# A four-layer graph network on one core: the program's end, the last group's gate and the due times of the planner rearranged

## The chip, the core and the metric

The kernel runs on one core of a Trainium2 chip. Its engines are TensorE (PE, with its weight loads shown apart as PEld), VectorE (DVE), ScalarE (ACT), GpSimd (POOL) and SyncE (SP), which issues the DMAs. The metric is the device time of one execution in microseconds. The kernel before takes 2499.73 us, the median of three runs (2499.19 to 2499.82).

## The reference

Input: 128 graphs of 64 nodes with 256 features (`x`), a 0/1 adjacency for each graph (`adj`) and a node mask. Four layers follow each other; each is `x = x + gnn(relu(layernorm(x)))`, and the layernorm has no weights of its own. Cut to what matters:

```python
# layers 0 and 1: attention, 8 heads of 32, masked by adj
scores = einsum('bhqd,bhkd->bhqk', q, k) / sqrt(32)        # layer 1 adds log(adj + 1e-6) instead
attn = softmax(where(adj > 0, scores, NEG))
out = merge_heads(attn @ v) @ Wo + bo
# layer 2: five GRU steps on h
for l in range(5):
    agg = A.T @ (h @ weight[l])
    r, z, n = gates(agg @ w_ih.T + b_ih, h @ w_hh.T + b_hh)
    h = (1 - z) * n + z * h
# layer 3: a gate between a neighbour part and an own part
f_hom = (adj @ ((x @ theta) * norm)) * norm                # norm = degree ** -0.5
f_het = x @ W_h
gate = sigmoid(x @ W_t + b_t)
out = elu(gate * f_hom + (1 - gate) * f_het)
```

All of it is float32.

## The kernel before, in words

Two graphs make a pair of 128 rows (tokens on the partitions); four pairs make a group, and there are 16 groups. For each group the function `front` computes layers 0 and 1 (in two halves of two pairs), `entry` and `gru` the five steps of layer 2 on all four pairs, and `back` (with `back_half` at L1453 for each half) layer 3. Dense products of two halves use a scheme with seven products in place of eight; the weights' combinations are made once at the start. Small products inside a graph (scores `s`, attention times values `o`, aggregation `agg`) use parts of the PE array: 64x64 or 64x32 tiles. Full products and transposes use all of it.

Nothing is issued in the order of the program text. Each operation is first added to a `Plan` with its engine, a cost in ns, what it reads and writes, and a due time. `plan.strand(base, span)` spreads the due times of the operations added in it evenly by PE cost over `base` to `base + span`, counted in groups. `Plan.run` then simulates five engine clocks and takes, again and again, the operation that can start first; among those that can start within 15 ns of the first it takes the one due first. Three sets of constants steer this:

- `AFTER`, `TO_PE`, `TO_POOL` and `EASE` say how long after an operation's end its result is there for another engine. `EASE` is a slack on top of all of them.
- `BESIDE`, `ALONE` and `TURNING` shift the due time of small-tile operations and transposes by the tile mode in which PE was left last (`shift`), and `AHEAD` limits how far ahead of the earliest due time an operation may be taken.
- `FRONT...`, `BACK...`, `STEP...`, `LOCK`, `ENTRY`, `FIRST...` and `FUSE...` are the bases and spans of the strands. `..._LAST` and `BACK_END` shift those of the last group or the last two, and `LOCK` starts the last group's layer 2 earlier.

The plan decides the order on each engine. On the chip each engine works through its own queue in that order and waits on semaphores.

Layer 3 in `back_half`, for each pair: the last state of layer 2 is added into `x` (L1458), `normed` makes the normalized and transposed `hT` (`lnT`, L563, is its transpose on PE; `st`, `mv`, `pw` and `rstd` are its statistics), products give `F` with three parts (L1396 and L1400 in `plain_products`: `f` on its own bank, `gate` with 512 columns for the gate and the own part). Then the bias is added to the gate (L1476 on POOL in the last group, L1479 on DVE in the others), tanh by ACT (L1481), `hom` by PE (L1483), three operations of DVE that combine the parts (L1486, L1489, L1491), the lower branch of ELU (L1497 by ACT in the last two groups, a min by DVE in the others, then exp at L1502), and two DVE operations that add both branches and the −1 into `x` (L1504, L1506). One DMA stores both pairs of the half (L1508, 256 KB).

The network exists in the program twice. The first copy (`flag` given, "lean") takes the softmax without subtracting the maximum and counts in `sure` and `once` whether that was safe (L1559 to L1577, which writes `flag`). The second copy is the fallback without this shortcut. Which one holds is decided at the end of the first (L284, L285):

```python
        network(tc, a, out, flag)
        beyond = nc.values_load(flag[0:1, 0:1])
        with tc.If(beyond > 0, preferred_fallthrough_block=False):
            network(tc, a, out, None)
```

With these inputs the fallback isn't run; each engine jumps over it. The wait for the last stores stands at the program's very end (L1607).

Of the kernel before, what the change touches and what calls it, by code (L numbers as in the profile page):

```python
# [23 lines left out]
P = 128  # L24
# [14 lines left out]

AFTER = {"PE": 210, "DVE": 125, "ACT": 145, "POOL": 90, "SP": 2500}  # L40
TO_PE, TO_POOL = 120, 60
EASE = 60


HOLD = {"DVE": 60, "POOL": 95}
# [5 lines left out]

WIDE, T64, T32, TURN = range(4)
CHANGE = ((0, 95, 95, 0), (290, 0, 170, 190), (250, 135, 30, 150), (0, 95, 95, 0))
BESIDE = 0.78
ALONE = 0.07
TURNING = 0.14
AHEAD = 1.25

FRONT = 0.1
FRONT_LAST = 0.25
FRONT_SPAN = 1.03
BACK = 0.0
BACK_LAST = 0.35
BACK_SPAN = 0.7
STEP = 0.1
STEP_LAST = -0.02
STEP_SPAN = 0.35
LOCK = 0.26  # L70
BACK_END = 0.1
ENTRY = 0.55
FIRST = -1.33
FIRST_SPAN = 1.08
ORDER = (0, 0, 1, 0, 1, 0)
FUSE = -1.25
FUSE_SPAN = 0.2


WEIGH = (655, 1147)  # L80
# [10 lines left out]
def dve(n, ptr=0):  # L91
    return n * 1.042 + 68 + 60 * ptr
# [186 lines left out]
def gnn_stack_kernel(tc: tile.TileContext, a: dict, out: bass.AP):  # L279
    nc = tc.nc  # L280
    with tc.tile_pool(name="flag", bufs=1) as keep:
        flag = keep.tile([P, 1], mybir.dt.int32, name="flag")
        network(tc, a, out, flag)
        beyond = nc.values_load(flag[0:1, 0:1])  # L284
        with tc.If(beyond > 0, preferred_fallthrough_block=False):  # L285
            network(tc, a, out, None)


# [1 line left out]
def network(ctx: ExitStack, tc: tile.TileContext, a: dict, out: bass.AP, flag):  # L290
# [38 lines left out]
    def vec2(cost, fn, reads, writes, early=0.0):  # L329

        plan.add("DVE", cost, fn, reads, writes, early=early, port=True)
# [4 lines left out]
    def pool(cost, fn, reads, writes, early=0.0, port=1):  # L336
        plan.add("POOL", cost, fn, reads, writes, early=early, port=port)
# [45 lines left out]
    def load_row(name):  # L383
        t = new(f"r_{name}", [P, D], 1)
        ap = a[name]
        dma(128, lambda: nc.sync.dma_start(
            t.tile, bass.AP(tensor=ap.tensor, offset=ap.offset, ap=[[0, P], [1, D]])), [], [t])
        return t
# [117 lines left out]
    with plan.strand(-0.3, 0.1):  # L506

        b_rz = new("b_rz", [P, 4], 1)
        vec(160, lambda: nc.vector.tensor_add(b_rz.tile, cols[:, 4:8], cols[:, 10:14]), [cols], [b_rz])
        vec(160, lambda: nc.vector.tensor_scalar(b_rz.tile, b_rz.tile, 0.5, None, op0=ALU.mult),  # L510
            [b_rz], [b_rz])


        b_n = new("b_n", [P, 2], 1)
        vec(160, lambda: nc.vector.tensor_sub(b_n.tile, cols[:, 8:10], cols[:, 14:16]), [cols], [b_n])


        w3 = new("w3", [P, 3, 8, P], 1)

        def load_w3():  # L520
            for i, name in enumerate(("L3_gnn_theta", "L3_gnn_W_t", "L3_gnn_W_h")):
                nc.sync.dma_start(w3[:, i, :4, :].rearrange("p (c o) q -> p c (o q)", c=2),
                                  a[name].rearrange("(c p) o -> p c o", p=P))

        dma(768, load_w3, [], [w3], 3)
        b_t = load_row("L3_gnn_b_t")


        b_row = new("b_row", [P, 2, 4, P], 1)
        more = new("e", [P, 2, 2, P], 4 if lean else 3, "b_more")  # L530

        def load_b():
            ih, hh = a["L2_gnn_b_ih"], a["L2_gnn_b_hh"]
            for dst, ap, at, gates in ((b_row[:, :, 0], ih, 2 * D, 0), (b_row[:, :, 3], hh, 2 * D, 0),
                                       (more[:, :, 0], hh, 0, 0), (more[:, :, 1], hh, D, 0),
                                       (b_row[:, :, 1], ih, 0, 0), (b_row[:, :, 2], ih, D, 0)):
                nc.sync.dma_start(dst, bass.AP(tensor=ap.tensor, offset=ap.offset + at, ap=[[0, P], [P, 2], [1, P]]))

        dma(768, load_b, [], [b_row, more], 6)
        pool(1225, lambda: nc.gpsimd.tensor_tensor(  # L540
            b_row[:, :, 1:3, :], b_row[:, :, 1:3, :], more.tile, op=ALU.add), [b_row, more], [b_row])
        blk = filled("adjblk", [P, PAIRS, P], 0.0)
# [911 lines left out]
    def back_half(g, xt, adjT, norm, half):  # L1454
        h_by_token = final[g]
        for p in range(2 * half, 2 * half + 2):
            t = g * PAIRS + p
            vec2(dve(256, 1), lambda t=t, p=p: nc.vector.scalar_tensor_tensor(  # L1458
                xt[:, p, :], h_by_token[:, p, :], cols[:, 18 + t : 19 + t], xt[:, p, :],
                op0=ALU.mult, op1=ALU.add),  # L1460
                [(h_by_token, ("half", half)) if g + 1 == n_groups else h_by_token, cols, (xt, p)], [(xt, p)])
        hT = normed(xt, half, f"{g}_3_{half}")

        F = [new("F" if g + 2 < n_groups or half else "h" if g + 2 == n_groups else ("kexp", "qk")[i], [P, 3, D], 2, f"F_{g}_{2 * half + i}") for i in range(2)]
        if g + 1 == n_groups or g + 2 == n_groups and not half:
            plain_products(hT, F, f"{g}_{half}")
        else:
            seven_products(hT, F, f"{g}_{half}")
        for p in range(2 * half, 2 * half + 2):
            nm = f"{g}_{p}"  # L1470
            v = F[p % 2]
            o = new("o", [P, D], 2, f"o3_{nm}")
            ph = bank(f"hom_{nm}")
            f, gt, het = (lambda k=k, v=v: v[:, k, :] for k in range(3))
            if g + 1 == n_groups:
                pool(650, lambda gt=gt: nc.gpsimd.tensor_tensor(gt(), gt(), b_t.tile, op=ALU.add),  # L1476
                     [(v, 0), (v, 1), b_t], [(v, "gt")])
            else:
                vec2(dve(256), lambda gt=gt: nc.vector.tensor_tensor(gt(), gt(), b_t.tile, op=ALU.add),  # L1479
                    [(v, 0), (v, 1), b_t], [(v, "gt")])  # L1480
            sca(act(256, 0.4), lambda gt=gt: nc.scalar.activation(gt(), gt(), AF.Tanh, scale=0.5),  # L1481
                [(v, "gt")], [(v, "gt")])
            pe(mm(256), lambda p=p, f=f, ph=ph: nc.tensor.matmul(  # L1483
                ph[:, :D], adjT[:, p, :], f(), start=True, stop=True), [adjT, (v, 0), (v, 1)], [ph], holds=[o])

            vec(dve(256, 1), lambda p=p, o=o, ph=ph, het=het: nc.vector.scalar_tensor_tensor(  # L1486
                o.tile, ph[:, :D], norm[:, p : p + 1], het(), op0=ALU.mult, op1=ALU.subtract),
                [ph, norm, (v, 0), (v, 1)], [o])
            vec2(dve(256), lambda o=o, gt=gt: nc.vector.scalar_tensor_tensor(  # L1489
                o.tile, gt(), 1.0, o.tile, op0=ALU.add, op1=ALU.mult), [(v, "gt"), o], [o])  # L1490
            vec2(dve(256), lambda o=o, het=het: nc.vector.scalar_tensor_tensor(  # L1491
                o.tile, o.tile, 0.5, het(), op0=ALU.mult, op1=ALU.add), [o, (v, 0), (v, 1)], [o])


            end = g + 2 >= n_groups
            if end:
                sca(act(256, 0.4), lambda o=o, gt=gt: nc.scalar.activation(gt(), o.tile, AF.Relu, scale=-1.0),  # L1497
                    [o], [(v, "gt")])
            else:
                vec2(210, lambda o=o, gt=gt: nc.vector.tensor_scalar(gt(), o.tile, 0.0, None, op0=ALU.min),  # L1500
                    [o], [(v, "gt")])
            sca(act(256, 0.4), lambda gt=gt, end=end: nc.scalar.activation(  # L1502
                gt(), gt(), AF.Exp, scale=-1.0 if end else 1.0), [(v, "gt")], [(v, "gt")])
            vec2(dve(256), lambda o=o, gt=gt: nc.vector.scalar_tensor_tensor(  # L1504
                o.tile, o.tile, 0.0, gt(), op0=ALU.max, op1=ALU.add), [o, (v, "gt")], [o])
            vec2(dve(256), lambda p=p, o=o: nc.vector.scalar_tensor_tensor(  # L1506
                xt[:, p, :], o.tile, -1.0, xt[:, p, :], op0=ALU.add, op1=ALU.add), [o, (xt, p)], [(xt, p)])
        dma(256, lambda: nc.sync.dma_start(  # L1508
            out_t[:, g * PAIRS + 2 * half : g * PAIRS + 2 * half + 2, :], xt[:, 2 * half : 2 * half + 2, :]),
            [(xt, 2 * half), (xt, 2 * half + 1)], [])  # L1510

    held, chains, final = {}, {}, {}
    parts = {g: front(g) for g in range(n_groups)}
    with plan.strand(FIRST, FIRST_SPAN):
# [41 lines left out]
                back(g, *held.pop(g))  # L1558
    if lean:  # L1559
        with plan.strand(n_groups + 0.2, 0.1):  # L1560
            once = new("once", [P, 2 * n_groups * 2 + 2], 1)
            means = slice(0, 4 * n_groups)
            vec2(200, lambda: nc.vector.tensor_scalar(
# [9 lines left out]
                count[:1, :1], once[:, n + 1 : n + 2], few[:, parity_sum : parity_sum + 1], start=True, stop=True),  # L1573
                [once, (few, 4)], [count])
            vec(70, lambda: nc.vector.tensor_scalar(
                flag[0:1, 0:1], count[:1, :1], float(P), None, op0=ALU.not_equal), [count], [])
    plan.run()  # L1577


# [31 lines left out]
```

## Time and profile before

| | |
|---|---|
| median of three runs | 2499.73 us |
| the profiled execution, its own time | 2500.02 us |
| its span, first to last instruction | 2498.1 us |
| mean granted PE clock | 0.996 |
| busy PE / DVE / ACT / POOL | 99% / 77% / 52% / 40% |
| PE's share of the chain that ended last | 97% |
| PE busy in 300 to 2100 us | 1800.0 of 1800 |
| PE busy in 0 to 20 us | 17.16 of 20 |
| PE busy in 2460 to 2487 us | 20.26 of 27, clock 0.87 |
| last DVE operation | starts 2490.77, takes 0.42 |
| issue of the last store | 2491.22, landed 2.9 us later |

The span is what the profiler saw between the first and the last instruction; 1.9 us of the execution's time lie around it. The page's slices of the span show the granted clock at nine tenths or more everywhere but in the last slice:

```profile
PE   9999999999999999999999999999999999999997
DVE  5567787878777787877878778787877878867777
PEclk9999999999999999999999999999999999999998
```

Each digit is a fortieth of the span (62 us). Where PE stands at 9, another engine's idle time costs nothing; what isn't at 9 is the end, in the last slice. Smaller gaps of PE, in the first slices too, are below what these digits show, so stretches of the trace have to be asked one by one.

### The profile page before, as it was taken

The page shows a single profiled execution, that of the slowest core. Times are in us where ns is not written, and L with a number is a line of the kernel's source. Part 1 is how long each engine was busy: PE and PEld are TensorE (multiplying, and loading weights), DVE is VectorE, ACT ScalarE, POOL GpSimd, SP SyncE. Part 2 cuts the span into 40 slices and gives each one's busy share as a digit, 9 for nine tenths or more (in the row PEclk, how much of TensorE's full clock was granted, in tenths as well). Part 3 has the DMA queues.
Part 4 walks back from the last instruction along what each step waited for, and adds up shares of the span by engine and source line. Part 5 has one row for each costly group of instructions (what it writes and reads, how often), then busy time and mean ns, then how long its engine had stood idle before and what let it go on. Part 6 is the DMA issues. An engine that isn't in the chain of part 4 may idle for free.

```text
span 2498.1 us, 58019 instructions
## 1 busy us (share of the span) xinstructions
PE 2472.3 (99%) x23481; PEld 2030.7 (81%) x23481; DVE 1911.6 (77%) x4524; ACT 1300.1 (52%) x2634; POOL 1009.7 (40%) x959
## 2 busy tenths in 40 slices
PE   9999999999999999999999999999999999999997
PEld 7788888887878878788888888878788787887874
DVE  5567787878777787877878778787877878867777
ACT  3355555555555555455555555555554555654544
POOL 5633424435243352533535244352433525234342
PEclk9999999999999999999999999999999999999998
DMA  7422212212222121222213132122222212212210
GB/s 219 155 81 86 75 50 95 77 50 87 72 80 70 62 83 63 80 70 84 76 48 104 50 102 74 55 77 72 80 70 69 73 62 80 74 49 70 72 50 19
DMA packets 88603, 191.45 MB, mean 77 GB/s; under 512 B 23603, under 2 KB 77189, under 8 KB 77445
## 3 DMA queue, kind: packets, MB, share of 16 engines
q1 hardware_dynamic: 88208, 187.59, 22.5%
q8 instruction: 188, 3.08, 0.5%
q14 instruction: 91, 0.74, 0.1%
q10 hardware_dynamic: 116, 0.04, 0.0%
HBM read 169.58 MB, written 18.02 MB: 75 GB/s over the span
## 4 chain that ended last, share of the span: by engine, by line
PE 97%; DVE 2%; ACT 1%; POOL 0%; issue 0%; DMA 0%; DVEq 0%; ACTq 0%
PE gb L1013 18%; PE gc L1013 13%; PE nb L1013 9%; PE nc L1013 7%; PE qkvb L727 6%; PE qkvc L727 5%; PE y L895 4%; PE nb L1195 3%; PE agg L1058 3%; PE gb L1195 3%; PE l3b L1425 3%; PE s L791 3%; PE gc L1195 3%; PE nc L1195 2%; PE l3c L1425 2%; PE hT L563 2%
## 5 line engine op out<-in xcount | busy, mean ns | idle before, releaser
L1127 POOL TENSOR_TENSOR sn<-h,sn 128x512 f32<-128x512 f32 x128 | 164.4, 1284 | 542.2 <-ACT sn L1125 542.2
L815 POOL TENSOR_TENSOR e<-e,mask 128x512 f32<-128x512 f32 x128 | 170.2, 1342 | 237.9 <-ACT e L813 237.9
L982 POOL TENSOR_TENSOR Th<-h 128x256 f32<-128x256 f32 x160 | 125.5, 803 | 272.4 <-PE nb L1013 133.1
L1013 PE MATMUL gb<-Ta,gv 128*128 128x256 f32 x768 | 199.0, 381 | 0.3 <-DVE Ta L1071 0.3
L1013 PE MATMUL gb<-Th,w_hh 128*128 128x256 f32 x768 | 197.4, 380 | 0.7 <-DVE sg L1090 0.7
L549 POOL TENSOR_TENSOR rstd<-pw,few 128x2 f32<-128x2 f32 x128 | 114.2, 892 | 206.3 <-DVE pw L548 202.9
L1013 PEld LDWEIGHTS gb<-Ta,gv 128*128 128x128 f32 x768 | 141.5, 190 | 21.9 <-DVE Ta L1071 0.7
L1125 ACT ACTIVATE sn<-sn,b_n 128x512 f32<-128x512 f32 x128 | 92.1, 720 | 129.1 <-DVE sn L1123 127.6
L1013 PEld LDWEIGHTS gb<-Th,w_hh 128*128 128x128 f32 x768 | 140.3, 190 | 20.1 <-issue 1.2
L1071 DVE TENSOR_TENSOR Ta<-agg 128x256 f32<-128x256 f32 x160 | 93.9, 589 | 79.5 <-ACT sg L1117 37.0
L1129 DVE SCALAR_TENSOR_TENSOR sn<-sg,sn 128x512 f32<-128x512 f32 x128 | 115.8, 905 | 45.9 <-POOL sn L1127 45.1
L982 POOL TENSOR_TENSOR Th<-h,Th 128x256 f32<-128x256 f32 x160 | 134.9, 843 | 8.9 <-DVE h L1131 5.9
L895 PE MATMUL y<-w_L_gnn_Wo,oT 128*128 128x256 f32 x512 | 133.3, 380 | 0.1
L1013 PE MATMUL gc<-h,w_hh 128*128 128x256 f32 x512 | 131.9, 380 | 0.1
L1013 PE MATMUL gc<-agg,gv 128*128 128x256 f32 x512 | 131.4, 379 | 0.0
L804 POOL TENSOR_TENSOR x<-x,r_L_gnn_bo 128x512 f32<-128x512 f32 x64 | 89.4, 1397 | 77.9 <-DVE xn L593 52.5
L568 ACT ACTIVATE hT<-lnT 128x512 f32<-128x512 f32 x96 | 57.2, 596 | 116.9 <-PE lnT L563 116.9
L1064 ACT ACTIVATE agg<-agg 128x512 f32<-128x512 f32 x160 | 86.6, 593 | 58.9 <-PE agg L1058 58.8
L1013 PE MATMUL nb<-Th,w_hh 128*128 128x256 f32 x384 | 116.1, 384 | 0.0
L1013 PE MATMUL nb<-Ta,gv 128*128 128x256 f32 x384 | 114.5, 380 | 0.0
L727 PEld LDWEIGHTS qkvb<-hTQ,qw 128*128 128x128 f32 x696 | 100.0, 191 | 16.6 <-DVE v L748 0.8
L1090 DVE TENSOR_TENSOR sg<-gc,ug 128x512 f32<-128x512 f32 x64 | 43.8, 685 | 89.4 <-PE gc L1013 88.2
(286 smaller groups left out, 7122.9 us busy)
## 6 DMA issues: line engine op xcount, KB each, us to landing
gv<-gates SPq DMA_DIRECT2D x80, 1344.0 KB, 5.8
qw<-kept SPq DMA_DIRECT2D x203, 192.0 KB, 2.4
x<-in_x_dram SPq DMA_DIRECT2D x32, 256.0 KB, 3.6
out_dram<-x SPq DMA_DIRECT2D x32, 256.0 KB, 2.2
gates<-gv SPq DMA_DIRECT2D x5, 1344.0 KB, 5.1
adjq<-in_adj_dram SPq DMA_DIRECT2D x8, 256.0 KB, 3.5
adjblk<-in_adj_dram SPq DMA_DIRECT2D x32, 64.0 KB, 2.3
gw<-in_L_gnn_weight_dram SPq DMA_DIRECT2D x5, 256.0 KB, 6.8
```

The source lines that it names most:

```text
L549: pool(660 if n == 2 else 970, lambda: nc.gpsimd.tensor_tensor(dst.tile, s.tile, few[:, 1 : 1 + n], op=ALU.pow), [s, (few, 1)], [dst], port=2)
L727: nc.tensor.matmul(bk[:, j * P : (j + 1) * P], lhs, rhs, start=first and j == 0, stop=True, skip_group_check=True)
L815: pool(1225, lambda e=e: nc.gpsimd.tensor_tensor(e.tile, e.tile, bias_at(pp)[:, None, :].to_broadcast([P, 4, 2 * NODES]), op=ALU.mult), [e ...
L895: pe(mm(256), lambda i=i, c=c: nc.tensor.matmul(py[:, i * D : (i + 1) * D], oT[:, i, c, :], w_o[:, c, :], start=c == 0, stop=c == 1), [(oT ...
L982: pool(690, lambda: nc.gpsimd.tensor_tensor(T[:, i, :], x(), y(), op=ALU.subtract), reads, [(T, i)])
L1013: nc.tensor.matmul(bank_[:, col * HALF : (col + 1) * HALF], at(g, n), rhs(), start=first and j == 0, stop=True, skip_group_check=True)
L1071: vec2(dve(256), lambda: nc.vector.tensor_tensor(Ta[:, i, :], x(), y(), op=ALU.subtract), reads, [(Ta, i)])
L1125: sca(act(TOK, 1.5), lambda: nc.scalar.activation(a_(), a_(), AF.Tanh, bias=b_n[:, oc : oc + 1]), [n_v, b_n], [n_v])
L1127: pool(1230, lambda: nc.gpsimd.tensor_tensor(b_(), hh(), a_(), op=ALU.subtract), [*hp, n_v], [n_v])
L1129: vec2(dve(TOK), lambda: nc.vector.scalar_tensor_tensor(b_(), z(), 1.0, b_(), op0=ALU.add, op1=ALU.mult), [*ts[1], n_v], [n_v])
L1195: pe(mm(384), lambda t=t, bk=bk: nc.tensor.matmul(bk[:, P:] if of_h else bk[:, : 3 * P], b()[:, t * P : (t + 1) * P], w[:, :, n, :], start ...
L1425: pe(mm(384), lambda: nc.tensor.matmul(bk[:, : 3 * P], b(), w3[:, :, n, :], start=first, stop=True, skip_group_check=True), [w3, *reads], ...
```

## The change

Four things change together.

1. The constants: `EASE` goes from 60 to 90 ns, and the mode shifts, the bases and spans of the strands get new values. These change the order on every engine, not what is computed.
2. The program's end. The last group's second half stores its two pairs one by one, 128 KB each. The last of these stores is an operation of its own, `last_store`: it loads the flag's value first and then issues the store. `network` hands the value back, and the branch stands right behind. `preferred_fallthrough_block=True` puts the fallback's block and the end block in another order: the jump to the far block is taken at the branch, and the block behind it stands next to the end.
3. The gate of the last group: the sigmoid's two parts come apart. ACT makes `part = 0.5 - 0.5 t` of the tanh `t` and `norm * (t + 1)`, POOL multiplies the own part by `part`, and DVE keeps one product and one addition. In the other groups the three DVE operations stay.
4. ELU. It is written as `max(o, 0) + min(exp(o), 1) - 1`. Both branches are added into `x` directly, so that the operation for `min(o, 0)` goes in every group (DVE's min, or ACT's relu in the last two). The −1 is no longer added in layer 3: `bo_1`, the bias of layer 1's output, is made smaller by 1 once at the start. The layernorms between don't see a shift that is the same in all features, and the residual carries it to the end.

Since every line after the first edits is shifted, so are the line numbers. The diff, cut to its core:

```diff
-EASE = 60
+EASE = 90
...
-BESIDE = 0.78
-ALONE = 0.07
-TURNING = 0.14
-AHEAD = 1.25
...
-FRONT = 0.1
-FRONT_LAST = 0.25
-FRONT_SPAN = 1.03
-BACK = 0.0
-BACK_LAST = 0.35
+BESIDE = 0.49
+ALONE = -0.01
+TURNING = 0.38
+AHEAD = 0.95
...
+FRONT = 0.07
+FRONT_LAST = 0.33
+FRONT_SPAN = 0.98
+BACK = -0.03
+BACK_LAST = 0.2
 BACK_SPAN = 0.7
 STEP = 0.1
-STEP_LAST = -0.02
-STEP_SPAN = 0.35
-LOCK = 0.26
-BACK_END = 0.1
-ENTRY = 0.55
-FIRST = -1.33
-FIRST_SPAN = 1.08
+STEP_LAST = 0.06
+STEP_SPAN = 0.3
+LOCK = 0.37
+BACK_END = 0.14
+ENTRY = 0.59
+FIRST = -1.15
+FIRST_SPAN = 0.78
 ORDER = (0, 0, 1, 0, 1, 0)
-FUSE = -1.25
-FUSE_SPAN = 0.2
+FUSE = -1.53
+FUSE_SPAN = 0.26
...
-        network(tc, a, out, flag)
-        beyond = nc.values_load(flag[0:1, 0:1])
-        with tc.If(beyond > 0, preferred_fallthrough_block=False):
+        beyond = network(tc, a, out, flag)
+        with tc.If(beyond > 0, preferred_fallthrough_block=True):
             network(tc, a, out, None)
...
+        bo_1 = attn[1][1]
+        vec2(210, lambda: nc.vector.tensor_scalar(bo_1.tile, bo_1.tile, -1.0, None, op0=ALU.add), [bo_1], [bo_1])
...
+        last, tail = g + 1 == n_groups, g + 1 == n_groups and half == 1
+        def one(p):
...
+            if last:
+                part = new("cp", [P, D], 5, f"part_{nm}")
+                sca(act(256, 0.4), lambda: nc.scalar.activation(part.tile, gt(), AF.Copy, scale=-0.5, bias=0.5),
+                    [(v, "gt")], [part])
+                pool(690, lambda: nc.gpsimd.tensor_tensor(part.tile, het(), part.tile, op=ALU.mult), [part, *all_of], [part])
+                sca(act(256, 2), lambda: nc.scalar.activation(
+                    gt(), gt(), AF.Identity, scale=norm[:, p : p + 1], bias=norm[:, p : p + 1]),
+                    [(v, "gt"), norm], [(v, "gt")])
+                vec(dve(256), lambda: nc.vector.scalar_tensor_tensor(
+                    o.tile, ph[:, :D], 0.5, gt(), op0=ALU.mult, op1=ALU.mult), [ph, (v, "gt")], [o])
+                vec2(dve(256), lambda: nc.vector.tensor_tensor(
+                    o.tile, o.tile, part.tile, op=ALU.add), [o, part], [o])
             else:
-                vec2(210, lambda o=o, gt=gt: nc.vector.tensor_scalar(gt(), o.tile, 0.0, None, op0=ALU.min),
-                    [o], [(v, "gt")])
-            sca(act(256, 0.4), lambda gt=gt, end=end: nc.scalar.activation(
-                gt(), gt(), AF.Exp, scale=-1.0 if end else 1.0), [(v, "gt")], [(v, "gt")])
-            vec2(dve(256), lambda o=o, gt=gt: nc.vector.scalar_tensor_tensor(
-                o.tile, o.tile, 0.0, gt(), op0=ALU.max, op1=ALU.add), [o, (v, "gt")], [o])
-            vec2(dve(256), lambda p=p, o=o: nc.vector.scalar_tensor_tensor(
-                xt[:, p, :], o.tile, -1.0, xt[:, p, :], op0=ALU.add, op1=ALU.add), [o, (xt, p)], [(xt, p)])
...
+            sca(act(256, 0.4), lambda: nc.scalar.activation(gt(), o.tile, AF.Exp), [o], [(v, "gt")])
+            vec2(dve(256), lambda: nc.vector.scalar_tensor_tensor(
+                xt[:, p, :], o.tile, 0.0, xt[:, p, :], op0=ALU.max, op1=ALU.add), [o, (xt, p)], [(xt, p)])
+            vec2(dve(256), lambda: nc.vector.scalar_tensor_tensor(
+                xt[:, p, :], gt(), 1.0, xt[:, p, :], op0=ALU.min, op1=ALU.add), [(v, "gt"), (xt, p)], [(xt, p)])
...
+        if tail:
+            dma(128, lambda: nc.sync.dma_start(out_t[:, g * PAIRS + p, :], xt[:, p, :]), [(xt, p)], [])
+            ends.append((xt, p + 1))
+            if not lean:
+                last_store()
+            return
...
+    def last_store(known=None):
+        xt, p = ends.pop()
+
+        def go():
+            if lean:
+                read.append(nc.values_load(flag[0:1, 0:1]))
+            nc.sync.dma_start(out_t[:, n_pairs - PAIRS + p, :], xt[:, p, :])
+
+        dma(128, go, [(xt, p)] + ([known] if lean else []), [])
...
-                flag[0:1, 0:1], count[:1, :1], float(P), None, op0=ALU.not_equal), [count], [])
+                flag[0:1, 0:1], count[:1, :1], float(P), None, op0=ALU.not_equal), [count], [known])
+        with plan.strand(n_groups + 2.0, 0.1):
+            last_store(known)
     plan.run()
+    return read[0] if lean else None
```

## The prediction

> **What bounds the kernel now.** The page's busy time and chain of waits come first: TensorE (PE) is busy 99% and carries 97% of the chain, so only three things count: what PE has to do, what it waits for, and what runs after its last matmul.
>
> ```profile
> PE 2472.3 (99%) x23481; PEld 2030.7 (81%) x23481; DVE 1911.6 (77%) x4524; ACT 1300.1 (52%) x2634; POOL 1009.7 (40%) x959
> PE 97%; DVE 2%; ACT 1%; POOL 0%; issue 0%; DMA 0%; DVEq 0%; ACTq 0%
> ```
>
> Next the busy time by stretches (stretch, length, PE busy, the other engines, clock):
>
> ```profile
> 300.00:2100.00 1800.00, 1800.00 (x17518) 1492.19 (x17517) 1416.62 (x3385) 966.58 (x1977) 721.47 (x671) 1.00 0.22 73
> 2460.00:2487.00 27.00, 20.26 (x62) 11.77 (x60) 20.76 (x57) 11.26 (x22) 4.77 (x6) 0.87 0.06 21
> 2487.00:2498.10 11.10, 0.00 (x1) 0.00 (x0) 3.85 (x10) 2.01 (x5) 0.57 (x1) 0.60 0.11 33
> ```
>
> The 1800 us of the steady groups have no idle PE; a gain there must come from the matmuls themselves. The waits lie in the first 300 us and the last 200. PE runs from 1.35 to 2486.4 = 2485.1 us. Adding up all its passes by their spacing in the trace (0.216 us for 256 columns) and the mode changes below gives 2458.8, so about 26.3 us are waits or slow clock: 7.3 in the start up to 20 us, 9.5 between 20 and 2455, 9.7 in 2460 to 2481. The waits by releaser name them, and the chain shows that the largest is a VectorE (DVE) chain:
>
> ```profile
> PE lnT L563 <- DVE xn L593: 4.8, 3, 3.4
> PE hom L1483 <- DVE F L1403: 2.4, 1, 2.4
> PE gb L1013 <- ACT agg L1064: 0.6, 1, 0.6
> ```
> ```profile
> 2465.57 0.31 DVE F L1403
> 2465.88 0.60 DVE sn L1260
> 2466.47 0.09 DVE mv L588
> 2466.56 0.37 DVE o L1486
> 2466.93 0.60 DVE sn L1265
> 2467.53 0.09 DVE pw L548
> 2467.69 1.76 POOL rstd L549
> 2469.47 0.42 DVE xn L593
> ```
>
> DVE pieces stand back to back: the third layer's normalization is late because DVE serves other tiles first.
>
> The matmul timeline shows what a change of tile shape costs:
>
> ```profile
> 2132.05 1.03 PE L1013 MATMUL gb<-Ta,gv 128*128 128x256 f32 x4
> 2133.01 0.45 PE L859 MATMUL o<-e,v 64*32 64x64 f32 x32
> 2134.30 1.10 PE L791 MATMUL s<-kexp,qk 64*64 64x128 f32 x32
> 2135.33 0.70 PE L1013 MATMUL nb<-Th,w_hh 128*128 128x256 f32 x2
> 2135.87 0.81 PE L1013 MATMUL gc<-h,w_hh 128*128 128x256 f32 x3
> ```
>
> From start to start, gb's four passes take 0.96 us instead of 4 x 0.216 = 0.86: entering small tiles costs 0.09. nb's two take 0.54 instead of 0.43: leaving them to a full product costs 0.10. Leaving to transposes costs 0.056 (seen at 2023.5), small to small nothing.
>
> Last, the program's end (duration in ns, first and last start):
>
> ```profile
> L285 SPq COMPARE_BRANCH  x2: 43/46/49, 2492.2 to 2494.2; - x2
> L1607 SPq EVENT_SEMAPHORE  x10: 17/28/28, 2496.8 to 2498.1; - x10
> out_dram<-x SPq DMA_DIRECT2D x2, 256.0 KB, 2.9
> ```
>
> SyncE (SP) issues the last store at 2491.22, loads the flag, waits for the landing (2.87), branches at 2494.23, and its next instruction starts at 2496.80: jumping over the fallback network takes 2.57 us after everything has landed.
>
> [...]
>
> **The change part by part.** All sums are against the profiled execution, 2500.02 us (span 2498.1 and 1.9 around it), 0.29 over the median.
>
> *Constants of the order.* The new EASE (90 for 60 ns) and due times leave the same 12,321 matmuls but order them differently. Comparing the two programs' PE orders: small-tile clusters entered from full tiles fall from 163 to 155, 8 x 0.093 = 0.74 us; exits to full products fall from 118 to 78 and those to transposes rise from 45 to 77: 118 x 0.104 + 45 x 0.056 = 14.79 against 78 x 0.104 + 77 x 0.056 = 12.42, so 2.37. Sum −3.11.
>
> *Waits in the middle.* I took the PE work that stands between a producer's end and its first use. agg of group 15, step 2: 0.49 us before (it waited 0.765), over 1.36 after; agg of group 1: 0.97 to over 1.36 (waited 0.287); hT_1_1_0 0.22 to 0.86 (0.632); oT_0_1_1 2.05 to 2.70 (0.245); kexp_1_1_0 2.21 to over 3.3 (0.329); Ta_15_3 5.29 to over 6.5 (0.452). These six go: −2.71. Of the other 6.8 the orders don't show that they go; taken at 0. Bounds: −3.5 (half go) to +4 (as many new ones appear; in the steady groups one distance shrinks, kexp of layer 1, 3.75 to 3.34 us against some 1.85 needed).
>
> *DVE's work.* A gate's min or relu, the −1 and the last add become two adds into x: one op fewer for each of 56 pairs in groups 0 to 13 (56 x 0.34 = 19 us of DVE), and one Relu fewer on ScalarE (ACT) for each pair of group 14. The −1 of ELU is now subtracted once in layer 1's output bias. All this lies beside full PE, so nothing; if DVE were the bound, it would be the 19. One small DVE op on bo_1 is added in the setup: nothing.
>
> *DVE chain ahead of the last normalization.* By the order, F_14_0's copy moves ahead of the chain's start (0.34) and one 0.60 op moves behind pw: lnT_15_3_0 comes 0.94 us earlier. The half-clock stretch moves with it. Bounds 0 and −2.5 [...].
>
> *The last group's gate.* After the last gate product (2486.14), before: DVE ends at 2491.19, 5.05 later. After, worked through with the trace's durations: ACT copy of 512 to +0.64, scaling by ACT +1.1 for the other pair, POOL add to 1.43 (0.72), tanh to 1.89 (0.42), part to 2.34, scaling by norm to 3.1, DVE product to 3.6, add to 4.0, exp to 4.47, last DVE op to 4.9. DVE has 4 ops for 5 per pair, but ACT's queue of five 0.42 ops for two pairs is now on the path. −0.15, bounds −0.6 and +0.7. It adds waits of DVE's product for ACT's scaling; behind it only the pair's own add stands.
>
> *The end.* SP stores pair 2 (128 KB), loads the flag, waits, stores pair 3 (128 KB) and branches at once; the far target now lies between the store's issue and its landing, and the block after it is adjacent. From DVE's last op to the end block: before 2496.80 − 2491.19 = 5.61. After: issue and branch 0.5, jump 2.57, then waits for the queues eight times 0.07 plus 0.1: 3.73; the landing at 0.03 + 2.87 = 2.9 is covered by the jump, the flag's load (0.48) by DVE's work; DVE's own far jump reaches 3.9, under SP's end. −1.88. Bounds: the jump takes DVE's 3.4: −1.05; the adjacent block's jump also fetches: +0.6.
>
> Sum: 3.11 + 2.71 + 0.94 + 0.15 + 1.88 = 8.79. 2500.02 − 8.79 = 2491.2; from the median, 2499.73 − 8.79 = 2490.9. I take 2491.0.
>
> **The rivals.** 0.2% is 5.0 us, about what a measurement can tell: faster is below 2494.7, slower above 2504.7.
> - *As summed*, 2491.0, own range 2488.5 to 2494.0: 0.55.
> - *The waits move*: the 2.71 isn't gained and up to 4 us come anew, for PE waits on semaphores alone rise from 639 to 740 in the order. 2491.0 + 2.7 + 4 = 2497.7, no change: 0.17. Against: the smallest distance of agg goes from 0.49 to 1.21.
> - *The jump isn't hidden* (it doesn't do what it says): if the end block is fetched anew. 2491.0 + 1.88 + 0.6 = 2493.5: 0.10.
> - *The other waits fall too*: half of 6.8, 3.5 us: 2487.5: 0.12. For it: the median distance of agg goes from 1.78 to 3.86.
> - *A wait in every steady group* (slower): the scores of layer 1's second half come before kexp, whose ACT op stands in ACT's queue; the distance is 3.34 us. It decides from (2504.7 − 2491.0) / 12 = 1.14 us per group, that is when kexp is ready 4.5 us after its product. At 1.25 us, 2491 + 15 = 2506: 0.06. Against: it now takes about 1.85.
>
> **How the numbers follow.** The first, third and fourth case are faster (0.77), the second no change (0.17), the fifth slower (0.06). Range 2487.5 to 2496.5: it takes in the first, third and fourth and two thirds of the second.
>
> **What would show it.** Steady groups should repeat every 151.08 us instead of 151.37, without idle PE. agg's wait in group 15 should be gone from the waits; PE's end near 2479. xn of the last group should come about 1 us sooner relative to the chain's start. SP's far branch should stand beside the last store, with no gap of 2.5 us after the landing. If PE shows idle time between 300 and 2100 us, the fifth case holds; if the end block comes over 5 us after DVE's last op, the third.

## The result, and the profile after

The changed kernel takes 2503.18 us, the median of 20 runs (2499.73 to 2507.52); the kernel before, run beside it, 2499.06 (2498.38 to 2500.01). The ratio is 1.0018, with a 95% interval of 1.0011 to 1.0025: slower by 4.1 us, where 8 us less were forecast. How far single runs lie apart is as telling: 7.8 us, those of before 1.6.

The profiled execution is one of the longer ones, 2507.30 us with a span of 2505.5, 7.4 over the span of before. In the busy time by stretches of the changed kernel (stretch, length, then busy time of PE, PEld, DVE, ACT, POOL, the granted clock, DMA) the gain and the loss stand apart:

```profile
20.00:97.00 77.00, 76.69 (x943) 58.62 (x942) 45.40 (x124) 26.87 (x51) 50.88 (x48) 1.00 0.56 183
97.00:175.00 78.00, 77.72 (x840) 68.10 (x839) 58.27 (x148) 41.11 (x82) 39.05 (x39) 1.00 0.31 107
175.00:300.00 125.00, 125.00 (x1194) 106.42 (x1192) 84.44 (x190) 64.45 (x128) 48.76 (x47) 1.00 0.20 68
300.00:2100.00 1800.00, 1788.70 (x17380) 1487.76 (x17382) 1423.90 (x3318) 955.29 (x1964) 712.38 (x666) 1.00 0.22 73
```

PE's idle time between 20 and 300 us is 0.6 us where it was 2.2 (0.60, 1.50 and 0.12 in the same stretches of before): the waits that were to go have gone. But the steady groups, without idle PE before, now have 11.3 us of it. Cut into stretches of one group's length, they show that it isn't the same in each:

```profile
1659.72:1810.80 151.08, 150.29 (x1463) 124.65 (x1462) 120.68 (x282) 80.80 (x166) 60.62 (x57) 1.00 0.22 73
1810.80:1961.88 151.08, 147.97 (x1453) 123.75 (x1452) 115.85 (x271) 79.27 (x163) 56.46 (x55) 0.99 0.22 73
1961.88:2112.96 151.08, 151.08 (x1468) 125.72 (x1467) 120.70 (x283) 80.72 (x166) 61.62 (x58) 1.00 0.22 73
```

Who ends these waits? The waits of PE by releaser, in the changed kernel (total us, times, longest):

```profile
PE o L860 <- issue: 7.4, 5, 3.1
PE lnT L564 <- DVE xn L594: 5.1, 4, 3.3
PE hom L1481 <- DVE mv L589: 2.3, 1, 2.3
```

The last two are those of before. The first is new, and its releaser is "issue": PE waited for nothing that a semaphore shows. (One more of the kind, the 2.3 us at 612 us, stands in this view as a wait for `hT` on ACT; its place in PE's instructions, below, shows what it is.) The longest of the five, in the timeline of PE:

```profile
1826.87 1.16 PE L1059 MATMUL agg<-A,ht 64*64 64x64 f32 x64
1827.96 0.45 PE L860 MATMUL o<-e,v 64*32 64x64 f32 x32
1828.23 0.78 PE L868 MATMUL o<-e,ones 64*32 64x256 f32 x16
1828.66 0.59 PE L860 MATMUL o<-e,v 64*32 64x64 f32 x25
1832.37 0.31 PE L860 MATMUL o<-e,v 64*32 64x64 f32 x7 [3.11 <-issue]
1832.61 0.66 PE L564 MATMUL lnT<-ident,xn 128*128 128x128 f32 x4
```

PE stops after 25 of 32 equal matmuls of one cluster and goes on 3.1 us later with the other 7. All 32 use the same tiles, so missing data is an unlikely reason. What is missing is the instructions. The trace's queue 8 brings packets of 16,384 bytes, of kind instruction, one for some 254 instructions of PE on average (188 packets for some 47,700), and counting PE's records from the start, 36,289 stand ahead of the one at which it goes on, that is 193 + 141 x 256.

A stop is counted from here on where the next matmul starts over 0.4 us later than matmuls of these two shapes usually follow each other; from start to start the longest is 3.3 us, 0.2 more than its idle time in the views. Between 300 and 2100 us there are nine, of 0.4 to 3.3 us, 12.9 in all. All nine end at 193 or 194 over a multiple of 256, each 2.2 to 3.1 us after the start of a packet of queue 8. So the instructions come in blocks of 256 here, with an edge at 193, and at these nine edges PE had used up one block before the next one was there.

What is in the way of the fetch shows beside it. SP issues a gv load at 1825.01 (1344 KB), and the DMA view of 1824 to 1834 us (the slices are 0.25 us) has the DMA engines nearly full until 1829.75, 0.5 us after PE stopped:

```profile
DMA  0000000992914999989999870002000000000030
...
q1 hardware_dynamic: 144, 1.38, 39.5%
q8 instruction: 2, 0.03, 1.4%
```

The instruction packet starts only at 1829.99, as the load runs out, takes 0.94, and PE goes on 1.4 us after its end.

This stop has a tail: a little after it the granted clock is half for 3.41 us (the same columns, the clock is the third from the end):

```profile
1826.89:1830.30 3.41, 2.36 (x138) 2.13 (x137) 1.91 (x3) 3.41 (x7) 1.06 (x1) 1.00 0.83 349
1830.30:1833.72 3.42, 1.35 (x14) 1.22 (x15) 1.00 (x3) 0.89 (x2) 1.26 (x1) 1.00 0.04 8
1833.72:1837.13 3.41, 3.41 (x12) 2.24 (x15) 2.63 (x10) 1.37 (x3) 0.00 (x0) 0.50 0.01 2
```

After the stop at 612 us (2.3 us idle) the clock is half from 615.16 to 618.57, and gc's four passes at 615.50 take 1.85 us from start to start, where the prediction has 4 x 0.216 = 0.86 at full clock. So 3.41 us at half the clock do the work of 1.7, and each such stretch loses 1.7 us more, in time that counts as busy. The groups agree: from its adjT transposes to the next group's, a group without a stop takes 150.83 us, the two groups with these stops 155.81 and 154.90.

Why so often after, and never before? Clusters of small tiles hold many instructions in little time: agg 128 in 1.09 us, o 160 in 1.29. Beside each other they use up a block of 256 in 2.1 us. In PE's order such pairs have gone from 13 to 39 (the kernel before sets o beside s instead, 32 times, which is 224 instructions in 2.3 us), and stretches of 256 instructions that take under 2.3 us, wherever they begin, from some 500 to some 1,400. Counted at the true block edges, with a gv load called in flight if it was issued up to 6 us before the fetch that ends the stop began:

```
300 to 2100 us       blocks under 5 us  stops  sum us  gv in flight: stops  sum us  longest us
before                       5            0      0                     0      0        -
the new end alone            5            0      0                     0      0        -
changed kernel              18            9     12.9                   6     10.1     3.3
new constants alone         16            6      9.8                   4      7.6     3.0
changed, 12 transposes      16            6      8.4                   4      6.2     2.8
agg and o kept apart         8            3      4.3                   3      4.3     1.8
gv in three DMAs            16            6      7.1                   5      5.9     1.8
gv in six DMAs              16            7      6.0                   3      2.6     1.5
```

Each row is one profiled execution. Six of the changed kernel's nine stops follow a block that ran for 2.0 to 2.7 us, the other three one of 4.5, 4.7 and 8.2 us, all three with a gv load in flight. In the kernel before, no block that meets a gv load (issued in it, or up to 6 us before it begins) is shorter than 6.4 us; in the changed one ten are. A fetch starts later beside the load in both kernels: 2.7 and 2.6 us after the block edge, as the median, against 1.3 elsewhere. Why the block of 8.2 us ran dry all the same isn't shown.

The rows below "changed kernel" are experiments, as is the new end alone. The program's end did what it was to do. The branch's own line in the changed kernel (duration in ns, first and last start):

```profile
L284 SPq EVENT_SEMAPHORE  x8: 17/17/17, 2503.6 to 2504.1; - x8
...
L284 SPq COMPARE_BRANCH  x1: 45/45/45, 2500.7 to 2500.7; - x1
```

And the last lines of its timeline:

```profile
2499.88 0.42 DVE L1507 SCALAR_TENSOR_TENSOR x<-F,x 128x256 f32<-128x256 f32 x1
2500.33 0.35 SPq L1537 DMA_DIRECT2D out_dram<-x  x1
```

SP branches 0.05 us after the last store is issued, and its next instruction starts 2.79 us later: the jump runs while the store lands (the eight waits behind the jump take 0.5 us in all, so none of them is held up by the store any more). From the end of DVE's last operation (2500.31) to the end of the span it takes 5.19 us, where before it took 6.93.

### The profile page after: what moved, and what is told of

It reads as the page before. It is cut to its first block, busy times and chain, and to the rows that moved or that the text cites. A ratio compares the mean times of both kernels' runs of the same rounds, so it can differ in the third digit from the quotient of the medians.

```text
span 2505.5 us, 58204 instructions
## 1 busy us (share of the span) xinstructions
PE 2471.4 (99%) x23481; PEld 2035.2 (81%) x23481; DVE 1926.4 (77%) x4465; ACT 1295.7 (52%) x2634; POOL 1011.1 (40%) x963
## 4 chain that ended last, share of the span: by engine, by line
PE 96%; DVE 2%; ACT 1%; issue 1%; POOL 0%; DMA 0%; DVEq 0%; ACTq 0%; POOLq 0%
PE gb L1014 17%; PE gc L1014 13%; PE nb L1014 9%; PE nc L1014 7%; PE qkvb L728 6%; PE qkvc L728 5%; PE y L896 4%; PE agg L1059 3%; PE gb L1196 3%; PE nb L1196 3%; PE l3b L1426 3%; PE s L792 3%; PE nc L1196 2%; PE lnT L564 2%; PE gc L1196 2%; PE hT L564 2%
## 5 line engine op out<-in xcount | busy, mean ns | idle before, releaser
L550 POOL TENSOR_TENSOR rstd<-pw,few 128x2 f32<-128x2 f32 x128 | 104.2, 814 | 204.0 <-DVE pw L549 197.8
L983 POOL TENSOR_TENSOR Th<-h,Th 128x256 f32<-128x256 f32 x160 | 142.2, 889 | 7.9 <-DVE h L1132 4.1
L1130 DVE SCALAR_TENSOR_TENSOR sn<-sg,sn 128x512 f32<-128x512 f32 x128 | 105.7, 826 | 45.9 <-POOL sn L1128 45.8
L896 PE MATMUL y<-w_L_gnn_Wo,oT 128*128 128x256 f32 x512 | 140.6, 383 | 0.0
L594 DVE TENSOR_SCALAR xn<-x,mv,rstd 128x256 f32<-128x256 f32 x192 | 114.6, 624 | 17.6 <-ACT ht L598 10.0
L896 PEld LDWEIGHTS y<-w_L_gnn_Wo,oT 128*128 128x128 f32 x512 | 95.2, 190 | 25.0 <-DVE oT L882 1.0
L1072 DVE TENSOR_TENSOR Ta<-agg 128x256 f32<-128x256 f32 x160 | 84.9, 551 | 33.8 <-ACT sg L1118 21.0
L1014 PEld LDWEIGHTS gc<-agg,gv 128*128 128x128 f32 x512 | 98.3, 192 | 13.6
```

The lines of the kernel that those rows point to most:

```text
L550: pool(660 if n == 2 else 970, lambda: nc.gpsimd.tensor_tensor(dst.tile, s.tile, few[:, 1 : 1 + n], op=ALU.pow), [s, (few, 1)], [dst], port=2)
L594: vec2(325, lambda p=p, i=i: nc.vector.tensor_scalar(xn[:, i, :], xt[:, p, :], mv_at()[:, i, 0:1], rstd[:, i : i + 1], op0=ALU.subtract, o ...
L896: pe(mm(256), lambda i=i, c=c: nc.tensor.matmul(py[:, i * D : (i + 1) * D], oT[:, i, c, :], w_o[:, c, :], start=c == 0, stop=c == 1), [(oT ...
L983: pool(690, lambda: nc.gpsimd.tensor_tensor(T[:, i, :], x(), y(), op=ALU.subtract), reads, [(T, i)])
L1014: nc.tensor.matmul(bank_[:, col * HALF : (col + 1) * HALF], at(g, n), rhs(), start=first and j == 0, stop=True, skip_group_check=True)
L1130: vec2(dve(TOK), lambda: nc.vector.scalar_tensor_tensor(b_(), z(), 1.0, b_(), op0=ALU.add, op1=ALU.mult), [*ts[1], n_v], [n_v])
```

## The experiments

Each was run in five rounds beside the kernel before, whose median in these runs lay between 2498.8 and 2499.4 us. The first four part the change.

**The new end alone.** The kernel before with `last_store`, the flag ahead of it and the branch with the far block behind it:

```diff
-        network(tc, a, out, flag)
-        beyond = nc.values_load(flag[0:1, 0:1])
-        with tc.If(beyond > 0, preferred_fallthrough_block=False):
+        beyond = network(tc, a, out, flag)
+        with tc.If(beyond > 0, preferred_fallthrough_block=True):
...
+        with plan.strand(n_groups + 2.0, 0.1):
+            last_store(known)
```

> Kernel before with only the new end of the program (last half stored pair by pair, flag loaded ahead of the last store, far jump beside it). PE's order is that of before. Theory (the end itself gains, as the trace of the changed kernel has it: 5.2 us from DVE's last operation to the span's end instead of 6.9): 2499.1 - 1.7 = 2497.4 us, runs within 2 us of each other as before. Rival (the near jump fetches too, nothing gained): 2499 to 2500.

Measured: 2497.12 us (2496.41 to 2498.65), ratio 0.9992 (0.9984 to 1.0001), the kernel before 2499.37. The medians differ by 2.2 us, where 1.7 was expected, and the runs stay together; by the interval the gain isn't beyond doubt. Its trace has 5.56 us from DVE's last operation to the end, 1.4 less than before. The branch stands 0.6 us behind the last store's issue here, not 0.4.

**The new constants alone.**

```diff
-EASE = 60
+EASE = 90
...
-BESIDE = 0.78
-ALONE = 0.07
-TURNING = 0.14
-AHEAD = 1.25
+BESIDE = 0.49
+ALONE = -0.01
+TURNING = 0.38
+AHEAD = 0.95
```

(and all bases and spans of the strands, as in the change)

> Kernel before with only the new constants. Theory A (PE's instruction fetch: agg and o clusters beside each other use up 256 instructions in 2.1 us, and a fetch that comes late behind a gv load stops PE): no gain of 5.8 us but 2503.2 - 2.8 (tail of the gate) + 1.7 (end) = 2502.1 us, single runs spread over 5 us or more, stalls of 1 to 3 us in the steady groups that no semaphore explains. Theory B (the constants gain as forecast, the gate's tail and the end cost it all): 2499.1 - 3.1 - 2.7 = 2493.3 us, runs within 2 us.

Measured: 2505.16 us (2498.52 to 2507.78), ratio 1.0023 (1.0013 to 1.0032). The constants alone carry the loss and the spread; theory B is out by 12 us. PE stops at the places of the changed kernel. The waits of this trace:

```profile
PE o L859 <- issue: 5.1, 3, 2.8
...
PE hT L563 <- issue: 0.8, 1, 0.8
```

**The changed kernel with the old constants** (the same diff backwards).

> The changed kernel with the old constants (new end, new gate and ELU remain). Theory A: no stalls, runs within 2 us; before - 1.7 (end) + 2.8 (gate's tail) + 1 (PE order of this build has 1 us more in mode changes) = 2501.2 us. Theory B (gate and end carry the loss of the changed kernel): 2503 us or more, over before by 4 + 5.8.

Measured: 2499.05 us (2497.57 to 2501.25), ratio 1.0000 (0.9991 to 1.0008). No stop at a block edge in the steady groups. It is 2 us better than expected, which fits that the tail of the new gate isn't 2.8 us longer. That reading was wrong: the 2.8 came from taking the first pair's last gate product for the second's. From the true one (ending at 2494.86 in the changed kernel) DVE's last operation ends 5.45 us later, against 5.22 before.

**The changed kernel with the old gate** of the last group:

```diff
-            if last:
+            if False:
                 part = new("cp", [P, D], 5, f"part_{nm}")
```

> The changed kernel with the old gate in the last group (three DVE operations, POOL and ACT only as before). Theory A: the tail after the last gate product goes from 7.8 us to about 5, so 2503.2 - 2.8 = 2500.4 us, and the runs still spread over 5 us. Theory B: all of the loss goes, 2494 us. Rival for the tail (the longer tail comes from the order, not from the gate's form): 2503.

Measured: 2502.12 us (2497.74 to 2507.47), ratio 1.0010 (1.0002 to 1.0019). The spread stays. The medians differ by 1.1 us, less than single runs differ among themselves; the traces say 4.81 us for the tail in place of 5.45, so 0.6 for the new gate's form. But nothing of it is left at the end: with the old gate the last two stores come 1.0 us apart, the issue of the last one takes 1.2 us, and from DVE's last operation to the end it takes 6.01 us instead of 5.19. Neither the 2.8 of the one theory nor the loss of the other.

The next four ask what the stops hang on.

**Other block edges.** 12 warm-up transposes in place of 20 ahead of everything else, so that each later instruction of PE stands 16 places earlier and PE's order stays:

```diff
-            for _ in range(20):
+            for _ in range(12):
                 nc.tensor.transpose(warm[:, :P], ident.tile, ident.tile)
```

> The changed kernel with 12 warm-up transposes at the start in place of 20. PE's order is the same after them, but every later instruction stands 16 places earlier, so the 256-instruction fetch blocks are cut elsewhere. Theory A (fetch stalls): going through the changed kernel's trace with the block edges moved by 16, no edge is left at which the fetch is late; the stalls of the steady groups go, 2503.2 - 7 = 2496.2 us, and the runs lie within 3 us. Rival (the waits come from the order, as semaphores or from the DMA traffic whatever the block edges): 2503 us and a spread of 7 us as before.

Measured: 2502.02 us (2497.82 to 2505.39), ratio 1.0011 (1.0005 to 1.0018). The forecast of no late edge was wrong: six stops, 8.4 us in all, where the changed kernel's profile has 12.9 and that of the new constants alone 9.8. But they moved, and just as far as the edges did. The timeline of the same place:

```profile
1822.78 0.66 PE L860 MATMUL o<-e,v 64*32 64x64 f32 x32
1823.37 0.33 PE L564 MATMUL lnT<-ident,xn 128*128 128x128 f32 x1
1826.27 0.55 PE L564 MATMUL lnT<-ident,xn 128*128 128x128 f32 x3 [2.57 <-issue]
```

All 32 matmuls of the cluster run now, then one transpose, then PE stops: 7 matmuls and one transpose later than in the changed kernel, each with its weight load, that is 16 instructions. All six stops are again at 193 or 194 over a multiple of 256 by this kernel's own count. Waits that come from the order or from data would have stayed at the same matmul.

**The same with the old gate**, as a candidate.

> The changed kernel with the old gate of the last group and 12 warm-up transposes. Theory A: the profiled run with the old gate (2502.1 us) has 8 us of fetch stalls; without them 2494.0 us, under the kernel with the new end alone (2497.1). Rival: 2502 us.

Measured: 2502.62 us (2498.85 to 2507.17), ratio 1.0014 (1.0006 to 1.0022). No gain either; seven stops, at the edges.

**The same with the kernel before**, as a control.

> Control: the kernel before with 12 warm-up transposes. Theory A: its order has no block edge at which the fetch is late, with the edges moved neither, so nothing changes: 2499.1 us (within 0.7). Rival (fewer warm-up transposes are themselves a gain): lower by as much as in the changed kernel.

Measured: 2501.29 us (2499.61 to 2502.85), ratio 1.0010 (1.0004 to 1.0017): 2 us slower, which neither theory expected. The profiled run is the fastest of them (2499.61), has no idle PE between 300 and 2100 us, and doesn't show where the 2 us of the others are. This stays open, and with it what fewer warm-up transposes alone do in the two experiments above.

**gv in three DMAs.** The load of the same bytes, in packets of 3,584 in place of 10,752:

```diff
-            dma(1400, lambda l=l, gv=gv: nc.sync.dma_start(gv.tile, made[l].tile), [made[l]], [gv])
+            def load_gv(l=l, gv=gv):
+                for k in range(3):
+                    nc.sync.dma_start(gv[:, k], made[l][:, k])
+            dma(1400, load_gv, [made[l]], [gv])
```

> The changed kernel with each load of gv (1344 KB) as three DMAs of 448 KB, so with packets of a third of the size; the order on PE is the same. Theory A1 (the fetch is late because it stands behind gv's long packets): the five stalls beside a gv load shrink by half or more, 2503.2 - 4 = 2499 us. Theory A2 (the block runs out faster than any fetch can follow, the load matters little): 2503 us, stalls unchanged.

Measured: 2498.18 us (2496.27 to 2501.70), ratio 0.9997 (0.9989 to 1.0005): 5.0 us faster than the changed kernel by the medians, with PE's order and the edges untouched. The stop of 3.11 us of idle PE in the timeline above is 1.15 here, the longest of all is 1.5, and the clock stays full in the steady groups. The stops with a gv load in flight sum to 5.9 us instead of 10.1, a little less than the halving that was expected. The load beside the fetch is a cause.

**agg and o kept apart.** A rule in the planner, on the changed kernel with the old gate; `AGG` is a mode of its own for agg:

```diff
     def shift(last, mode, small):
+        if {last, mode} == {AGG, T32}:
+            return 0.3
```

> The changed kernel with the old gate of the last group, and with a rule in the planner that keeps agg and o clusters from standing beside each other (a due time 0.3 groups later for one right behind the other). In its order no stretch of 256 PE instructions takes under 2.3 us (1,464 such windows in the changed kernel, 490 in the one before), but mode changes cost 6.9 us more than in the changed kernel, 3.8 more than before. Theory A (bursts of instructions stop PE): no stall at a block edge and runs within 2.5 us; 2499.1 - 2.2 (end) + 3.8 - 2.7 (waits that the new constants take away) - 0.4 (tail) = 2497.6 us. Rival (the new due times bring the waits whatever stands beside what): 2502 + 6.9 = 2509 us, runs spread over 7 us.

Measured: 2516.01 us (2515.62 to 2517.05), ratio 1.0066 (1.0052 to 1.0079). The spread is gone (1.4 us, in five runs), the time is not: it is above both forecasts. There are still three stops at edges, after blocks of 3.2 to 4.3 us and with a gv load in flight, so blocks needn't run off in 2.1 us for the fetch to be late. The greater loss is another: small waits that come back in each group.

```profile
PE agg L1061 <- ACT hT L571: 2.9, 12, 0.2
...
PE o L862 <- ACT agg L1067: 2.1, 11, 0.2
```

With the mode changes, a group without a stop (from its adjT transposes to the next group's) takes 152.5 us, where the changed kernel has 150.8 and the one before 151.4. From start to start the two waits are 0.7 of the 1.7 us; the rest isn't taken apart. The experiment says that bursts aren't needed, and nothing on what they would cost alone.

**gv in six DMAs** (each third in two parts; packets of 2,048 and 1,536 bytes).

> The changed kernel with each gv load as six DMAs (packets of 2,048 and 1,536 B in place of 10,752; three DMAs with 3,584 gave 2498.2 us). If the length of the packets ahead of the fetch is what makes it late: as good or better, 2496 to 2498 us. If three DMAs helped for another reason (a later start of gv's bulk, luck with the block edges): no such step, 2500 us or more.

Measured: 2495.65 us (2492.73 to 2498.04), ratio 0.9986 (0.9979 to 0.9992), better than both kernels. The step goes on with the packets' size: 2503.2, 2498.2, 2495.7. Six issues also come 2.3 to 2.4 us apart from first to last, and the runs don't tell this spreading from the packets' length. There are seven stops, against nine, and none is over 1.5 us; those with a gv load in flight cost 2.6 us instead of 10.1, those without 3.4 instead of 2.8. Single runs still lie 5.3 us apart. PE's idle time in the steady groups is 5.4 us:

```profile
300.00:2100.00 1800.00, 1794.60 (x17504) 1492.91 (x17503) 1432.05 (x3335) 961.65 (x1977) 720.27 (x674) 1.00 0.24 74
```

**The new end with gv in three DMAs**, on the order of before.

> Control and candidate: the kernel before with the new end, and gv loaded in three DMAs. Its order has no late fetch in the steady groups, so the parts bring nothing there: 2497.1 us (within 0.6), as the new end alone. Rival (three DMAs help in themselves, in any order): 2493 us.

Measured: 2496.55 us (2496.03 to 2498.38), ratio 0.9992 (0.9984 to 1.0000), 0.6 below the new end alone: within what was expected. Where no fetch is late, smaller packets bring next to nothing. So most of the 5.0 us came from the fetches.

**gv in six DMAs with the old gate**, as the last candidate.

> Candidate: gv in six DMAs, new constants, new end, and the old gate of the last group (the trace with the old gate has 4.81 us from the last gate product to DVE's last operation, the new gate 5.45). If that adds up: 2495.65 - 0.6 = 2495.0 us. Rival (the gate's 0.6 us is lost in what the fetches do from run to run): 2495.7 or above.

Measured: 2495.55 us (2493.14 to 2498.04), ratio 0.9986 (0.9979 to 0.9992). No better than with the new gate. The tail is 4.81 us instead of 5.44, but from DVE's last operation to the end it now takes 5.78 instead of 5.18: the last two stores come 1.0 us apart instead of 1.8, and the issue of the last one takes 1.0 us instead of 0.35.

## Why the prediction was wrong, step by step

- **The step that failed** is the first reading: that the steady groups have no idle PE, so that "a gain there must come from the matmuls themselves", and that a change of order there is worth its mode changes and its semaphore waits. The 8 small-tile clusters that no longer follow a full tile were counted as gain alone ("small to small nothing"), and the fetch of PE's instructions stands in no term of the sum. What it costs isn't in any semaphore: side by side the clusters use up 256 instructions in 2.1 us, while a fetch starts 1.3 us after the block edge as the median, 2.6 beside a gv load, and PE goes on 2.2 to 3.1 us after the start of the packet. The profiled run shows 12.9 us of stops in the steady groups and 3.4 of half clock after two of them. It is one of the longer runs, so a run at the median will hold less of both.
- **The fetch was counted in the wrong place.** The prediction has it at the branch at the end only. In the kernel before, SP's next instruction comes 2.57 us after its branch and DVE's 3.4 us after its own (2491.6 to 2495.0), and two instruction packets start on queue 14 behind SP's branch, at 2495.2 and 2495.6; whose they are isn't shown. PE's stream has its own edges: 138 in the steady groups, without a stop in the kernel before, and with one at nine of them in the changed one. The measured 0.4 to 3.3 us at those decide.
- **The mode changes** were right in sign: groups without a stop repeat every 150.83 us, not 151.08, against 151.40 before. With the new constants alone it is 150.83 too. Over twelve groups that is 6.8 us, where the whole term was 3.11; why it is more, and whether all of it is mode changes, isn't shown.
- **The waits in the middle** went where they lie between 20 and 300 us (2.2 to 0.6 us). From 2300 to 2460 idle PE is 2.8 us against 2.4: agg's wait in group 15 is gone, but others came, of 0.5 and 0.8 us. Of the 2.71 some 1.6 were gained.
- **The DVE chain** ahead of the last normalization: from DVE's sum on gc's product to xn 9.86 us against 10.20. The two operations moved as read from the order (0.94), but POOL's rstd took 2.36 us instead of 1.76, as the chain of waits of the changed kernel shows. It takes so long in every trace with the new constants and 1.75 in every one with the old; why is open.

```profile
2474.73 0.09 DVE pw L549
...
2474.88 2.36 POOL rstd L550
...
2477.27 0.42 DVE xn L594
```

- **From the last normalization's transposes to the last gate product** it takes 17.0 us against 16.0, which the sum had left out. The order of the products isn't the cause: with gv in three DMAs, in the very same order, it is 15.6, and with the order of before and the new end 16.9. The clock is half for 10.2 us here, until 2485.7 (the gate products come 0.85 us apart, later 0.43), and for 6.8 in the kernel before (the granted clock is 0.52 in 2470.0 to 2475.9). In all fourteen traces the two go together: 15.6 to 16.0 us where the half clock lasts 6.8, 16.4 to 17.0 where it lasts 10.2. The prediction's bounds let this stretch go (its −2.5 was the author's estimate), but not grow.
- **The last group's gate**: 5.45 us against 5.22, so +0.2 where −0.15 was taken, inside its bounds. With the new gate the last two stores come 1.85 us apart and the end takes 5.2 to 5.3 us in five traces; with the old one they come 1.03 or 1.04 us apart, and it takes 5.25 to 6.65 in six.
- **The end**: −1.74 where −1.88 was taken.
- **The sum without the missing term** comes out near, and partly by luck: the profiled run with gv in six DMAs takes 2495.65 us, its median too, and has 6.0 us of stops left; 2495.65 − 6.0 = 2489.7, where 2491.0 was predicted. The mechanisms that the prediction named were there, but the order gave twice its term, the waits and the DVE chain about half of theirs, and up to 1.0 us was lost to the clock. A cost that the prediction didn't name took back more than they gave. (7.3, 9.5 and 9.7 us of waits add up to 26.5, not 26.3; nothing hangs on it.)
- **The rivals**: "the waits move" (2497.7) is 5.5 us off and had the wrong kind, as no semaphore is in the stops. "A wait in every steady group" (2506) is nearest to the measured 2503.18, and its sign, idle PE between 300 and 2100 us, came true with 11.3 us. Its cause didn't: kexp isn't among PE's waits in the trace, and three of the eleven whole groups have no stop at all. A sign that two causes share can't tell them apart. Small waits in each group are what the experiment that keeps agg and o apart ran into, for hT and agg.

## What to carry to other kernels

This kernel, with TensorE full, had a fourth thing to pay for beside work, waits and mode changes: its own instructions, 12.9 us of stops in 1800 us of the profiled run. Where hundreds of small matmuls stand side by side (here 256 instructions in 2.1 us), count instructions per microsecond, and look at which large DMA is in flight there (here one of 1344 KB). The signs here were waits whose releaser is "issue" in the middle of equal matmuls (up to 3.1 us), places that lie a whole number of 256 instructions apart, and single runs 7.8 us apart where the kernel before had 1.6. Splitting that DMA in six was the cheapest cure here, some 7.5 us for a loop around one line.

## What the runs showed of the hardware that was not expected

- An instruction packet of 16,384 bytes takes 0.9 to 1.8 us on its queue, and after a stop PE goes on 1.2 to 1.6 us after its end. Beside a gv load with 10,752 byte packets the fetch starts late enough to stop PE for up to 3.3 us; the block ahead of such a stop ran for 2.0 to 8.2 us.
- In these traces the length of a stop doesn't say whether the clock falls. In the steady groups it is half for 3.41 us or twice that, in stretches that begin a whole number of 3.41 us apart. Laid on that grid, half clock followed every stretch with PE busy for 1.35 us or less (six of them) and none with 1.75 or more. In between, one stop of 1.6 us (agg and o apart, the first two lines) brought the clock down, and one of 2.1 (the new constants alone, the last two) did not, the same 1.64 us of PE in both:

```profile
1376.96:1380.37 3.41, 1.64 (x80) 1.34 (x80) 2.30 (x7) 2.17 (x5) 1.62 (x1) 1.00 0.24 99
1380.37:1383.78 3.41, 3.41 (x9) 2.70 (x9) 2.15 (x7) 1.19 (x2) 0.00 (x0) 0.50 0.00 0
610.20:613.61 3.41, 1.64 (x8) 1.46 (x9) 2.73 (x9) 1.41 (x3) 1.27 (x1) 1.00 0.04 8
613.61:617.02 3.41, 3.41 (x44) 2.70 (x43) 2.13 (x4) 1.76 (x4) 0.87 (x1) 1.00 0.00 0
```

None of the stretches that half clock followed was idle throughout: PE was busy for 0.7 to 1.6 us in them.

- Two stores that are issued 1.03 to 1.04 us apart: the second issue took 0.35, 0.53, 0.62, 1.00, 1.03 and 1.17 us in six traces. At 1.85 us apart it took 0.35 in all five.
- What decides when a fetch starts isn't shown. In the steady groups of the kernel before, nine in ten packets of queue 8 start when PE is between 157 and 307 instructions past a multiple of 256, counted from the start (the block edge is at 193).
